# Tap weights from quarters of the TensorE array, kept in SBUF by ScalarE, with the products spread over the band

## The chip, the cores and the metric

One NeuronCore of a Trainium2 chip runs the whole kernel. The metric is the device time of one execution in microseconds. All data are float32.

## The reference, cut to what matters

Two layers work on an image batch x of 8 x 256 channels x 64 x 64. Each normalises x by groups (`_gn`) and adds its result to x. Layer 0 makes, for every pixel and every group of 8 channels, nine weights from a small network, and takes the weighted sum of the 3x3 neighbours of a value map x3. The change is in this layer:

```python
x1, x2, x3 = conv1x1(x, w1, b1), conv1x1(x, w2, b2), conv1x1(x, w3, b3)   # 32, 32, 256 channels
h = concat([x1, unfold3(reflect_pad(x2))])          # 32 + 9*32 maps
h = relu(bn2(conv1x1(relu(bn1(h)), cw1)))           # 32 maps
w = conv1x1(h, cw2, cb2).reshape(B, 32, 9, H, W)    # nine tap weights for each of 32 groups
x3u = unfold3(zero_pad(x3)).reshape(B, 32, 8, 9, H, W)
out = einsum('bgskhw,bgkhw->bgshw', x3u, w)         # 8 channels of a group share its weights
x = x + out
```

Layer 1 is a 7x7 local attention of four heads, plus a depthwise branch in which two depthwise 3x3 convolutions are weighted by a softmax over nine maps made from x (the matrix Wfc). It is left out here, since the change doesn't touch it.

## The kernel before

**Bands and steps.** An image is cut into 8 bands of 8 rows, so the batch has 64 bands. The main loop runs over g from -12 to 63. Pass g does layer 1 of band g, and, beside it, layer 0 of later bands: the maps of band g + 12 (`small_maps`, `value_maps`), the hidden maps of band g + 11 (`hidden_maps`), and the tap weights and products of band g + 10 (`tap_weights`). For g < -1 there is no layer 1 yet; the code calls these bands `alone`, and they are bands 0 to 8. The other 55 bands of tap weights are made beside layer 1, until g = 53. In the last ten passes layer 1 is alone.

**Order.** The whole order is written by hand (`manual_schedule`). A pass has 8 steps s, and a step has six places at which `advance()` runs what `after(n, f)` has deferred by n places; so a band has 48 places. Each engine executes its own queue in the order of issue. A pool tile with `bufs=n` is a ring: the next tile of that tag waits until the n-th before it has been read.

**Layer 0 in quarters.** For the tap weights a band of 8 rows is split into four quarters of 2 rows (SR = 2), and the 128 partitions are 4 quarters x 32 groups. h2 (the 32 hidden maps, `h2n`, two buffers, rows padded to HP = 66) therefore has 128 partitions x 132 elements. The weights matrix `c2` is block diagonal, four times the same 32x32 block, so that one 128x128 matmul per tap makes that tap's weights of all quarters:

```python
pw = ps.tile([P, n, SR * HP], F32, tag="gen", name=f"pw_{b}_{i}_{u}", bufs=4)
nc.tensor.matmul(pw[:, j], c2[:, first + j], h2n[i % 2]..., start=True, stop=True)
```

A matmul in float32 is two instructions, so a tap is two rows of the profile. Beside layer 1 the nine taps are made in five lots of 2, 2, 2, 2 and 1, at the end of steps 1 to 5 of the pass (`TAPS_AT`, `TG`). Each lot takes one of the four PSUM banks of tag `gen`, which it shares with most other results: pf (the Wfc maps, L886), ptp (transposed attention weights, L787), pq, pk, pv and p3. The score tiles sco (L750) and the tile small have banks of their own.

**Products.** One or two places after its lot, `product(j)` on VectorE (L483) adds the bias of tap k to its weight map in PSUM, and multiplies it, broadcast over the 8 channels of a group, with the shifted value map `x3q` in SBUF (128 x 1040). GpSimd then adds the product to `xg` (L491), which holds x. Products go through a ring of two tiles. After the ninth, VectorE takes statistics of xg, and it is written to DRAM as the input of layer 1.

**Other work on these engines.** VectorE also masks the scores (L764), makes the 8 other taps of each depthwise convolution (L843, L869, with their sums acc in PSUM), adds the attention results to xr (L818), and does the reciprocals of the softmax (L779, L907). GpSimd adds up the nine exponential maps (ex, L1106), and does the dynamic sum's other steps (L899, L902, L908, L912, L913). L912 and L913 read oc, the scaled depthwise result that ScalarE writes (L879), from a ring of two tiles. ScalarE makes all exponentials (L772, L891), empties most PSUM banks, and applies h2's Relu in `relu` (L441). DMAs beside layer 1 are issued by SP.

Of the kernel before, what the change touches and what calls it, by code (L numbers as in the profile page):

```python
# [10 lines left out]
F32 = mybir.dt.float32  # L11
BF16 = mybir.dt.bfloat16
AF = mybir.ActivationFunctionType
# [5 lines left out]
P = 128  # L19
C = 256  # L20
NCT = C // P
# [3 lines left out]
BAND = R * W  # L25
NB = H // R
# [4 lines left out]
REL = 32  # L31
KK = 9
# [3 lines left out]
SR = R // NQR  # L36
SHARE = C // REL
PIECE = SR * W
RUN = (SR - 1) * (W + 2) + W
TG = 2, 3  # L40
HP = W + 2
HR = R + 2

# [18 lines left out]
AHEAD = NB + 4  # L62
AHEAD0 = AHEAD + NB + 1
STEPS = NCT * NT // 2


TAPS_AT = (1, 2, 3, 4, 5), (0, 2, 4)
PRODUCTS_AT = ((1, 2),) * 5, ((7, 14, 10), (9, 17, 13), (12, 20, 16))


CB3, CBQ, CBK, CBP, CWP0, CWP1, CW1, CW2, CBV = 0, 1, 2, 3, 4, 5, 6, 15, 24
# [16 lines left out]
def conv_layers_kernel(ctx: ExitStack, tc: tile.TileContext, ins: dict, out: bass.AP):  # L88
    nc = tc.nc
    x_in = ins["x"]  # L90
    B = x_in.shape[0]

    const = ctx.enter_context(tc.tile_pool(name="const", bufs=1))
# [14 lines left out]
    def load(name, shape, src=None, now=True):  # L108
        t = const.tile(shape, F32, name=f"c_{name}")
        late.append(lambda: nc.scalar.dma_start(out=t, in_=ins[name] if src is None else src))  # L110
        if now:
            late.pop()()
        return t
# [8 lines left out]
    c1 = load("c1", [P, 3, REL])  # L122
    gq = load("gq", [P, P])
    gc = load("gc", [P, NCT, P])
    c2 = load("c2", [P, KK, P], now=False)
    wq = load("wq", [P, NCT, C], ins["wq"].rearrange("(t p) n -> p t n", p=P), now=False)
    wk = load("wk", [P, NCT, C], ins["wk"].rearrange("(t p) n -> p t n", p=P), now=False)
    wv = load("wv", [P, NCT, C], ins["wv"].rearrange("(t p) n -> p t n", p=P), now=False)
# [10 lines left out]
    x3n = [const.tile([P, R, HP], F32, name=f"x3n_{ct}") for ct in range(NCT)]  # L139

    h2n = [const.tile([P, SR, HP], F32, name=f"h2n_{i}") for i in range(2)]
    for t in probs + x3n + h2n:
        nc.gpsimd.memset(t, 0.0)

    def inverse_root(v):
# [45 lines left out]
    def layer1_loads():  # L191


        last = w1.tile([P, NCT, 1, C], F32, tag="oc", name="last")
        for f in late:
            f()
        nc.scalar.dma_start(out=last, in_=wfc_in[:, :, KK - 1 :])

        def first():
            nc.vector.tensor_scalar(wv, wv, rate1, None, ALU.mult)  # L200

        def difference(kt):
            nc.vector.tensor_sub(wfc[:, kt], wfc[:, kt], last[:, kt].to_broadcast([P, KK - 1, C]))

        return [first, lambda: difference(0), lambda: difference(1)]
# [205 lines left out]
    def hidden_maps(b, i, alone):  # L413

        im = images[b]
        hids = []
        h2 = h2n[i % 2][:, :, :W]

        def hidden(t):
            n = P if t == 0 else 96
            hid = w0.tile([P, R, W], F32, tag="hid", name=f"hid_{b}_{i}_{t}", bufs=2)
            nc.scalar.activation(
                hid[:n], im.x2[i][:n, t : t + R, :], AF.Relu, bias=bn1b[:n, t : t + 1], scale=bn1s[:n, t : t + 1]
            )
            hids.append(hid)

        def conv(home, first, last, start, stop):
            ph = home[:, 2 * P : 3 * P].rearrange("p (r c) -> p r c", r=SR)  # L430
            for t in range(first, last):
                n = P if t == 0 else 96
                for q in range(NQR):
                    nc.tensor.matmul(  # L434
                        ph[q * REL : (q + 1) * REL], c1[:n, t], hids[t][:n, q * SR : (q + 1) * SR],
                        start=(t == start), stop=(t == stop),
                    )
            return ph

        def relu(v):  # L440
            nc.scalar.activation(h2, v, AF.Relu, bias=bn2b, scale=bn2s)  # L441

        def one(home):
            ph = conv(home, 0, 2, 0, 1)
            after(1, lambda: hidden(2))
            after(2, lambda: nc.scalar.copy(h2, ph))

        def two(home):
            ph = conv(home, 2, 3, 2, 2)
            after(1, lambda: nc.vector.tensor_add(h2, ph, h2))  # L450
            after(3, lambda: relu(h2))

        hidden(0)
        after(3 if alone else 5, lambda: hidden(1))
        if alone:

            home = ps.tile([P, 4 * P], F32, tag="acc", name=f"ph_{b}_{i}")
            after(7, lambda: conv(home, 0, 2, 0, 2))
            after(8, lambda: hidden(2))
            after(12, lambda: after(4, lambda ph=conv(home, 2, 3, 0, 2): relu(ph)))  # L460
        return [two, one]

    def tap_weights(b, i, u, alone, at):


        im = images[b]
        first, n = TG[alone] * u, min(TG[alone], KK - TG[alone] * u)
        pw = ps.tile([P, n, SR * HP], F32, tag="gen", name=f"pw_{b}_{i}_{u}", bufs=4)
        for j in range(n):
            nc.tensor.matmul(  # L470
                pw[:, j], c2[:, first + j], h2n[i % 2].rearrange("p r c -> p (r c)"), start=True, stop=True
            )

        def product(j):
            k = first + j
            if alone and j == n - 1:
                prod = w1.tile([P, NCT, RP, W], F32, tag="yp", name=f"prod_{b}_{i}_{k}", bufs=3)
                prod = prod.rearrange("p t r c -> p (t r c)")[:, : SHARE * SR * HP]
                prod = prod.rearrange("p (s n) -> p s n", s=SHARE)
            else:  # L480
                prod = w0.tile([P, SHARE, SR * HP], F32, tag="prod", name=f"prod_{b}_{i}_{k}", bufs=2)
            at = k // 3 * HP + k % 3
            nc.vector.scalar_tensor_tensor(  # L483
                prod[:, :, :RUN], pw[:, j, :RUN].unsqueeze(1).to_broadcast([P, SHARE, RUN]),
                par[:, PCB2 + k : PCB2 + k + 1],
                im.x3q[i].rearrange("p s r c -> p s (r c)")[:, :, at : at + RUN], ALU.add, ALU.mult,
            )
            if alone and j == n - 1:
                after(9, lambda: gather(prod))
            else:  # L490
                nc.gpsimd.tensor_add(im.xg[i], im.xg[i], rows(prod))  # L491
            if k == KK - 2 + (not alone):
                if alone:
                    after(13, combine)
                after(14 if alone else 7, take)

        def rows(v):
            return v.rearrange("p s (r c) -> p s r c", c=HP)[..., :W]

        def gather(prod):  # L500
            if u == 0:
                im.part = score_tile(f"sum_{b}_{i}").rearrange("p t (s r c) -> p t s r c", r=SR, c=W)
            for t in range(2):
                nc.tensor.matmul(
                    im.part[:, t], ident, rows(prod)[:, t * SHARE // 2 : (t + 1) * SHARE // 2],
                    start=(u == 0), stop=(u == KK // n - 1),
                )

        def combine():
            x = im.xg[i].rearrange("p s r c -> p (s r c)")  # L510
            nc.vector.tensor_add(x, im.part.rearrange("p t s r c -> p (t s r c)"), x)

        def take():
            x = im.xg[i]
            if i == 0:
                im.st1 = stat.tile([P, 2 * NB, 6], F32, tag="st1", name=f"st1_{b}")
            for t in range(2):
                v = x[:, t * SHARE // 2 : (t + 1) * SHARE // 2].rearrange("p s r c -> p (s r c)")
                nc.vector.bn_stats(im.st1[:, 2 * i + t, :], v)
            im.x1[i] = dram.tile([C, BAND], F32, tag="x1", name=f"x1_{b}_{i}")  # L520
            if alone:
                after(9, lambda: keep(nc.scalar))
            else:
                keep(nc.sync)

        def keep(queue):
            for q in range(NQR):
                v = im.xg[i][q * REL : (q + 1) * REL].rearrange("p s r c -> p s (r c)")
                queue.dma_start(out=pieces(im.x1[i], q), in_=v)

        for j in range(n):
            after(at[j], lambda j=j: product(j))
# [133 lines left out]
    kept = {}  # L666
# [208 lines left out]

    def depthwise_end(b, i, ct, acc):

        oc = w1.tile([P, BAND], F32, tag="oc", name=f"oc_{b}_{i}_{ct}")
        nc.scalar.activation(oc, acc.rearrange("p r c -> p (r c)"), AF.Copy, scale=rate2)  # L879
        return oc  # L880

# [45 lines left out]
    def beside(g, s):  # L927
# [48 lines left out]
        alone = g < 0  # L976
# [8 lines left out]
        if 0 <= g + AHEAD - 1 < B * NB and s == (2 if alone else 1):  # L985
# [5 lines left out]
                    convs.extend(parts)  # L991

            end.append(hidden)
        if 0 <= g + AHEAD - 2 < B * NB and s in TAPS_AT[g < -1]:
            u = TAPS_AT[g < -1].index(s)
            end.append(
                lambda: tap_weights(*divmod(g + AHEAD - 2, NB), u, g < -1, PRODUCTS_AT[g < -1][u])
            )
        return head, mid, end

    def steer(g, s):
# [128 lines left out]
def _layout(inputs):  # L1130
# [29 lines left out]
    arr["par"] = par  # L1160

    c2 = a["a_cw2"].reshape(REL, KK, REL).transpose(2, 1, 0)
    arr["c2"] = np.zeros((P, KK, P), f)
    for q in range(NQR):
        arr["c2"][q * REL : (q + 1) * REL, :, q * REL : (q + 1) * REL] = c2

    chan = np.zeros((C, NCHAN), f)
    chan[:, CB3] = a["a_b3"]
# [43 lines left out]
```

## Time and profile before

| | |
|---|---|
| median of 3 runs | 3852.04 us (3850.59 to 3853.89) |
| profiled execution, its own time | 3854.63 us |
| its span in the profile | 3852.8 us |
| TensorE (PE) busy | 3756.3 us, 97% |
| VectorE (DVE) busy | 3434.4 us, 89% |
| GpSimd (POOL) busy | 3116.8 us, 81% |
| ScalarE (ACT) busy | 2809.2 us, 73% |
| mean granted TensorE clock | 0.994 |

Busy times are of one profiled execution. A group's row gives line, engine and operation, output and input by the program's names, shapes, the count, then busy time and mean nanoseconds of one, then the idle time of the engine in front of them with what ended most of it. In a timeline each row is a start, a length, the engine and the instructions that were merged into it. Bands are not marked in the profile: the steady part, with both layers at work, reaches from some 250 us to 3336 us.

### The profile page before, as it was taken

Reading aid. Unit: us, or ns where it says so; the run is one execution under the profiler, and the core shown is the slowest. Engines: PE = TensorE matmul, PEld = TensorE weight load, DVE = VectorE, ACT = ScalarE, POOL = GpSimd, SP = SyncE. Lnnn points to the kernel's source line nnn. Section 1 sums busy time; section 2 is a strip of 40 time slices with the busy share of each in tenths; the row PEclk is TensorE's granted clock in tenths of the full one; section 3 lists DMA queues with packets and bytes.
Section 4 is the critical chain, followed back from the end, with each engine's and each line's share of the span. In section 5 each row is a group of like instructions: output and inputs, shape, how many; then the busy total and the mean of one; then the engine's idle time right before and its main releaser. Section 6 shows DMA issues by size and latency. Waiting matters only on the chain.

```text
span 3852.8 us, 71646 instructions
## 1 busy us (share of the span) xinstructions
PE 3756.3 (97%) x24620; PEld 2109.9 (55%) x24620; DVE 3434.4 (89%) x7125; ACT 2809.2 (73%) x6770; POOL 3116.8 (81%) x2100
## 2 busy tenths in 40 slices
PE   6889999999999999999999999999999999999998
PEld 3445555555555555555555555555555555555554
DVE  6879999999999999899998999999999899978877
ACT  4457777777777777777777777777777777677776
POOL 4868888888897888888888888888888888855565
PEclk9999999999999999999999999999999999999999
DMA  8764544544444544544544544454544544232221
GB/s 247 210 177 128 142 118 129 151 126 118 133 135 131 145 123 115 148 135 127 136 116 142 142 125 120 126 149 125 136 115 117 138 119 114 74 97 78 79 67 37
DMA packets 438926, 490.14 MB, mean 127 GB/s; under 512 B 62016, under 2 KB 324256, under 8 KB 438304
## 3 DMA queue, kind: packets, MB, share of 16 engines
q1 hardware_dynamic: 421984, 469.79, 44.1%
q10 hardware_dynamic: 16576, 15.76, 1.3%
q8 instruction: 194, 3.18, 0.4%
q14 instruction: 172, 1.41, 0.1%
HBM read 343.76 MB, written 145.10 MB: 127 GB/s over the span
## 4 chain that ended last, share of the span: by engine, by line
PE 81%; POOL 10%; DVE 3%; DMA 2%; ACT 2%; issue 2%; SPq 1%; ACTq 0%; POOLq 0%; DVEq 0%
PE pf L886 39%; PE small L799 6%; PE ptp L787 6%; POOL xg L491 6%; PE pk L706 5%; PE pq L684 5%; PE sco L750 5%; PE p L375 5%; PE pv L601 5%; PE pw L470 2%; POOL ex L1106 2%; PE small L332 1%; DVE prod L483 1%; PE small L434 1%; DMA x<-x3n 1%
## 5 line engine op out<-in xcount | busy, mean ns | idle before, releaser
L886 PE MATMUL pf<-yp,c_wfc 128*128 128x512 f32 x4096 | 1916.8, 594 | 11.3 <-DVE prod L483 6.3
L491 POOL TENSOR_TENSOR xg<-xg,prod 128x1024 f32<-128x1024 f32 x549 | 1199.8, 2185 | 132.5 <-DVE prod L483 103.6
L886 PEld LDWEIGHTS pf<-yp,c_wfc 128*128 128x128 f32 x4096 | 739.6, 190 | 711.4 <-issue 654.7
L1106 POOL TENSOR_TENSOR ex<-ex,ex 128x1024 f32<-128x1024 f32 x384 | 908.8, 2367 | 68.5 <-ACT ex L891 65.0
L891 ACT ACTIVATE ex<-pf 128x512 f32<-128x512 f32 x1024 | 604.0, 590 | 347.9 <-PE pf L886 269.2
L843 DVE SCALAR_TENSOR_TENSOR acc<-yp,c_chan,acc 128x504 f32<-128x504 f32 (+3 forms) x1104 | 775.5, 702 | 63.2 <-ACT acc L834 42.8
L483 DVE SCALAR_TENSOR_TENSOR prod<-pw,c_par,x3q 128x1040 f32<-128x1040 f32 x576 | 732.7, 1294 | 107.9 <-PE pw L470 60.8
L869 DVE SCALAR_TENSOR_TENSOR acc<-hid,c_chan,acc 128x504 f32<-128x504 f32 (+3 forms) x1024 | 751.1, 733 | 18.1
L781 ACT ACTIVATE prob<-prob,tot 128x196 f32<-128x196 f32 x1024 | 412.9, 452 | 242.4 <-DVE tot L779 236.8
L772 ACT ACTIVATE prob<-prob,nmax 128x196 f32<-128x196 f32 x1024 | 458.2, 450 | 101.3 <-DVE nmax L764 101.2
L907 DVE RECIPROCAL rec<-tot 128x256 f32<-128x256 f32 x256 | 445.7, 1741 | 28.3 <-POOL tot L902 27.5
L789 ACT COPY pt<-ptp 112x512 f32<-112x512 f32 x511 | 295.9, 579 | 111.8 <-PE ptp L787 111.8
L764 DVE CUSTOM_DVE_ANT_0 prob<-sco,c_mask 128x196 f32<-128x196 f32 x1024 | 324.8, 355 | 31.0 <-PE sco L750 31.0
L787 PEld LDWEIGHTS ptp<-ident,prob 128*112 128x112 f32 x2044 | 227.3, 133 | 184.4 <-issue 132.7
L787 PE MATMUL ptp<-ident,prob 128*112 128x128 f32 x2044 | 319.5, 279 | 0.0
L908 POOL TENSOR_TENSOR tot<-tot,rec 128x256 f32<-128x256 f32 x254 | 185.8, 732 | 145.7 <-DVE rec L907 139.7
L799 PEld LDWEIGHTS small<-pt,vt 112*64 112x64 f32 x8144 | 258.6, 138 | 79.8 <-issue 60.5
L799 PE MATMUL small<-pt,vt 112*64 112x64 f32 x8144 | 294.2, 225 | 3.3 <-DMA vt<-vd 1.8
L601 PE MATMUL pv<-c_wv,yp 128*128 128x256 f32 x1056 | 253.5, 383 | 1.8 <-ACT yp L572 1.8
L902 POOL TENSOR_SCALAR tot<-tot 128x512 f32<-128x512 f32 x127 | 243.9, 1920 | 11.1
L470 PEld LDWEIGHTS pw<-h2n,c_c 128*128 128x128 f32 x1152 | 175.1, 191 | 139.9 <-issue 115.9
L375 PE MATMUL p<-xc,w3s 128*128 128x512 f32 x512 | 243.3, 598 | 0.0
(136 smaller groups left out, 4656.7 us busy)
## 6 DMA issues: line engine op xcount, KB each, us to landing
vt<-vd SPq DMA_DIRECT2D x512, 112.0 KB
x3q<-x SPq DMA_DIRECT2D x128, 264.0 KB
xc<-in_x SPq DMA_DIRECT2D x64, 512.0 KB
xg<-in_xg SPq DMA_DIRECT2D x64, 512.0 KB
yp<-x SPq DMA_DIRECT2D x128, 256.0 KB
xr<-x SPq DMA_DIRECT2D x64, 512.0 KB
out_x<-xr SPq DMA_DIRECT2D x64, 512.0 KB
xs<-in_x SPq DMA_DIRECT2D x57, 512.0 KB
```

Of the source, the lines that this page charges most:

```text
L483: nc.vector.scalar_tensor_tensor(prod[:, :, :RUN], pw[:, j, :RUN].unsqueeze(1).to_broadcast([P, SHARE, RUN]), par[:, PCB2 + k : PCB2 + k + 1],
L491: nc.gpsimd.tensor_add(im.xg[i], im.xg[i], rows(prod))
L601: nc.tensor.matmul(pv[:, g], yp[:, kt, r : r + 2].rearrange("p r c -> p (r c)"), wv[:, kt], start=(kt == 0), stop=(kt == NCT - 1),)
L772: nc.scalar.activation(prob[:, h, :NKEY], prob[:, h, :NKEY], AF.Exp, bias=nmax[:, h : h + 1], scale=-1.0, accum_out=tot[:, h : h + 1],)
L787: nc.tensor.transpose(ptp[:, h, ch], prob[:, h, ch * CHUNK : (ch + 1) * CHUNK], ident)
L799: nc.tensor.matmul(po[half[h], :, t * TQ : (t + 1) * TQ], im.vt[i + ch, m][:n, t, (2 * ct + h) * HD : (2 * ct + h + 1) * HD], pt[:n, h, ch ...
L843: nc.vector.scalar_tensor_tensor(o, yp[:, ct, ra + dr : rb + dr, ca + dc : cb + dc], chan[:, ct, CW1 + k : CW1 + k + 1], o, ALU.mult, ALU.add,
L869: nc.vector.scalar_tensor_tensor(o, hid[:, ra + dr : rb + dr, ca + dc : cb + dc], chan[:, ct, CW2 + k : CW2 + k + 1], o, ALU.mult, ALU.add,)
L886: nc.tensor.matmul(pf, wfc[:, kt, 2 * m + j, ct * P : (ct + 1) * P], images[b].yp[i][:, kt, PAD : PAD + R], start=(kt == 0), stop=(kt == N ...
L891: nc.scalar.activation(ex[:, j].rearrange("p (r c) -> p r c", r=R), pf, AF.Exp)
L907: nc.vector.reciprocal(rec, v)
L1106: after(4, lambda ex=ex, exb=exb: nc.gpsimd.tensor_add(ex, ex, exb))
```

## The change

The nine taps are made in two lots of 4 and 5 (`TAPS`), at the end of the last step of the pass before and of step 3 (`TAPS_AT`). Each matmul now uses a quarter of the array: 64 rows by 64 columns. A tap needs two of them, one for each half of its output partitions. Taps of a lot's first list use the upper 64 rows and write one PSUM bank, those of its second list use the lower 64 rows and write another, so that a tap needs both halves of h2 on the same 64 partitions. For that `relu` writes a second tile `h2s`, in which the halves of h2 are exchanged. `c2` shrinks to 64 columns.

Beside layer 1, ScalarE copies both banks of a lot to an SBUF tile `kept` (one buffer) one place later, and the products read their weights from there. They are spread over the band: 3, 8, 14 and 20 places after the first lot, 2, 5, 8, 11 and 14 after the second. For the 9 bands in front the products still read PSUM, at the places of before, and all their taps use the upper 64 rows.

The ring of tag `oc` goes from two tiles to one. In the diff, `...` marks what is left out.

```diff
-TG = 2, 3
+HALF = P // 2
...
-TAPS_AT = (1, 2, 3, 4, 5), (0, 2, 4)
-PRODUCTS_AT = ((1, 2),) * 5, ((7, 14, 10), (9, 17, 13), (12, 20, 16))
+TAPS = (((0, 1), (2, 3)), ((4, 5, 6), (7, 8))), tuple(((k, k + 1, k + 2), ()) for k in (0, 3, 6))
+TAPS_AT = (-1, 3), (0, 2, 4)
+PRODUCTS_AT = ((3, 8, 14, 20), (2, 5, 8, 11, 14)), ((7, 14, 10), (9, 17, 13), (12, 20, 16))
...
-    c2 = load("c2", [P, KK, P], now=False)
+    c2 = load("c2", [P, KK, HALF], now=False)
...
+    h2s = const.tile([P, SR, HP], F32, name="h2s")
-    for t in probs + x3n + h2n:
+    for t in probs + x3n + h2n + [h2s]:
         nc.gpsimd.memset(t, 0.0)
...
-        last = w1.tile([P, NCT, 1, C], F32, tag="oc", name="last")
+        last = w1.tile([P, NCT, 1, C], F32, tag="oc", name="last", bufs=1)
...
         def relu(v):
+            for a, z in ((0, HALF), (HALF, 0)):
+                o, z = slice(a, a + HALF), slice(z, z + HALF)
+                nc.scalar.activation(h2s[o, :, :W], v[z], AF.Relu, bias=bn2b[z], scale=bn2s[z])
             nc.scalar.activation(h2, v, AF.Relu, bias=bn2b, scale=bn2s)
...
-        first, n = TG[alone] * u, min(TG[alone], KK - TG[alone] * u)
-        pw = ps.tile([P, n, SR * HP], F32, tag="gen", name=f"pw_{b}_{i}_{u}", bufs=4)
-        for j in range(n):
-            nc.tensor.matmul(
-                pw[:, j], c2[:, first + j], h2n[i % 2].rearrange("p r c -> p (r c)"), start=True, stop=True
-            )
+        lots = TAPS[alone][u]
+        ks = [k for lot in lots for k in lot]
+        n = len(ks)
+        pws = [
+            ps.tile([P, len(lot), SR * HP], F32, tag="gen", name=f"pw_{b}_{i}_{u}_{r}", bufs=4)
+            for r, lot in enumerate(lots) if lot
+        ]
+        side = [slice(0, HALF), slice(HALF, P)]
+        for m in range(len(lots[0])):
+            for q in range(2):
+                for r, lot in enumerate(lots):
+                    if m < len(lot):
+                        h2 = (h2n[i % 2] if q == r else h2s)[side[r]].rearrange("p r c -> p (r c)")
+                        nc.tensor.matmul(pws[r][side[q], m], c2[side[r], lot[m]], h2, start=True, stop=True)
+        weights = [pw[:, m] for pw, lot in zip(pws, lots) for m in range(len(lot))]
+
+        def keep():
+            kept = w0.tile([P, KK - 4, SR * HP], F32, tag="pw", name=f"kept_{b}_{i}_{u}", bufs=1)
+            for pw, lot, at in zip(pws, lots, (0, len(lots[0]))):
+                nc.scalar.copy(kept[:, at : at + len(lot)], pw)
+            weights[:] = [kept[:, j] for j in range(n)]
+
+        if not alone:
+            after(1, keep)
...
             nc.vector.scalar_tensor_tensor(
-                prod[:, :, :RUN], pw[:, j, :RUN].unsqueeze(1).to_broadcast([P, SHARE, RUN]),
+                prod[:, :, :RUN], weights[j][:, :RUN].unsqueeze(1).to_broadcast([P, SHARE, RUN]),
                 par[:, PCB2 + k : PCB2 + k + 1],
                 im.x3q[i].rearrange("p s r c -> p s (r c)")[:, :, at : at + RUN], ALU.add, ALU.mult,
             )
...
-        oc = w1.tile([P, BAND], F32, tag="oc", name=f"oc_{b}_{i}_{ct}")
+        oc = w1.tile([P, BAND], F32, tag="oc", name=f"oc_{b}_{i}_{ct}", bufs=1)
...
-        if 0 <= g + AHEAD - 2 < B * NB and s in TAPS_AT[g < -1]:
-            u = TAPS_AT[g < -1].index(s)
-            end.append(
-                lambda: tap_weights(*divmod(g + AHEAD - 2, NB), u, g < -1, PRODUCTS_AT[g < -1][u])
-            )
+        for gt, st in ((g, s), (g + 1, s - STEPS)):
+            front = gt < -1
+            if 0 <= gt + AHEAD - 2 < B * NB and st in TAPS_AT[front]:
+                u = TAPS_AT[front].index(st)
+                end.append(
+                    lambda gt=gt, u=u, front=front: tap_weights(
+                        *divmod(gt + AHEAD - 2, NB), u, front, PRODUCTS_AT[front][u]
+                    )
+                )
```

More of the change, by code (lines that the diff above doesn't have):

```diff
@@ L466, in tap_weights @@
         im = images[b]
-        first, n = TG[alone] * u, min(TG[alone], KK - TG[alone] * u)
-        pw = ps.tile([P, n, SR * HP], F32, tag="gen", name=f"pw_{b}_{i}_{u}", bufs=4)
-        for j in range(n):
-            nc.tensor.matmul(
-                pw[:, j], c2[:, first + j], h2n[i % 2].rearrange("p r c -> p (r c)"), start=True, stop=True
-            )
+        lots = TAPS[alone][u]
[20 more added lines that the diff above has]
+            after(1, keep)
         def product(j):
-            k = first + j
+            k = ks[j]
             if alone and j == n - 1:
@@ L1162, in _layout @@
     c2 = a["a_cw2"].reshape(REL, KK, REL).transpose(2, 1, 0)
-    arr["c2"] = np.zeros((P, KK, P), f)
+    arr["c2"] = np.zeros((P, KK, HALF), f)
     for q in range(NQR):
-        arr["c2"][q * REL : (q + 1) * REL, :, q * REL : (q + 1) * REL] = c2
+        o = q * REL % HALF
+        arr["c2"][q * REL : (q + 1) * REL, :, o : o + REL] = c2
     chan = np.zeros((C, NCHAN), f)
```

## Prediction

> **What bounds the kernel now.** I read the page's busy line and chain first, to find the engine that sets the pace; then the windows of the steady part, for what the others have left.
>
> ```profile
> PE 3756.3 (97%) x24620; PEld 2109.9 (55%) x24620; DVE 3434.4 (89%) x7125; ACT 2809.2 (73%) x6770; POOL 3116.8 (81%) x2100
> PE 81%; POOL 10%; DVE 3%; DMA 2%; ACT 2%; issue 2%; SPq 1%; ACTq 0%; POOLq 0%; DVEq 0%
> PE pf L886 39%; PE small L799 6%; PE ptp L787 6%; POOL xg L491 6%; PE pk L706 5%; PE pq L684 5%; PE sco L750 5%; PE p L375 5%; PE pv L601 5%; PE pw L470 2%; POOL ex L1106 2%; PE small L332 1%; DVE prod L483 1%; PE small L434 1%; DMA x<-x3n 1%
> ```
>
> ```profile
> 1000.00:2000.00 1000.00, 994.98 (x6609) 563.01 (x6608) 921.46 (x1916) 757.33 (x1828) 855.78 (x575) 1.00 0.47 129
> 2000.00:3000.00 1000.00, 993.80 (x6682) 564.91 (x6681) 915.43 (x1910) 759.70 (x1838) 860.18 (x571) 1.00 0.48 131
> ```
>
> The windows' columns are busy time of PE, weight loads, DVE, ACT and POOL, then the granted clock. TensorE has 0.6% idle and is the bound. The tap weights (pw) are 2% of the chain. But DVE is at 92% and POOL at 86%. The group of the dynamic sum's first pass (L899 on POOL) starts first at 280.6 us, and the last pw matmul is at 3335.8, which is 53.3 bands later, so a band lasts **57.3 us**. Of that DVE has 4.7 us idle, POOL 8.1, ACT 13.8. The tail after 3336 us has no layer 0 work left. The change works on the 55 bands that are built beside layer 1; the 9 built in front keep products from PSUM.
>
> **What the Trainium skill says.** (1) "SBUF — State Buffer", section "Who interferes with whom": VectorE's second SBUF read goes through an interface that it shares with GpSimd. A VectorE instruction with two SBUF inputs and a GpSimd instruction that reads SBUF exclude each other for a whole instruction; one with at most one SBUF input does not contend. (2) "TensorEngine Tiling (Array Packing)", sections "Key Properties" and "Gotcha 1: PSUM Pressure": tiles run in parallel, different row tiles must write different PSUM banks, and a change of tiling mode drains the array.
>
> The trace agrees with (1). Nearly every long DVE row of this kernel has one operand in PSUM (pw, acc, sco, small, pk). The exception is L205, twice the same subtraction of 128x2048 from SBUF and SBUF. DVE first, then POOL:
>
> ```profile
> 55.60 4.20 DVE L205 TENSOR_TENSOR c_wfc<-c_wfc,last 128x2048 f32<-128x2048 f32 x1
> 71.55 2.28 DVE L205 TENSOR_TENSOR c_wfc<-c_wfc,last 128x2048 f32<-128x2048 f32 x1
> ```
>
> ```profile
> 50.97 6.68 POOL L491 TENSOR_TENSOR xg<-xg,prod 128x1024 f32<-128x1024 f32 x3
> 68.66 2.17 POOL L491 TENSOR_TENSOR xg<-xg,prod 128x1024 f32<-128x1024 f32 x1
> 75.19 11.23 POOL L491 TENSOR_TENSOR xg<-xg,prod 128x1024 f32<-128x1024 f32 x5 [4.36 <-DVE prod L483]
> ```
>
> The second runs 71.55 to 73.83, with POOL idle from 70.83 to 75.19: 2.28 us. The first starts while POOL is in the third of three additions, which ends at 57.65. It takes 4.20 us: 55.60 plus a wait to 57.52, plus 2.28. So it stood still until POOL was done. That is one case of DVE held by POOL; POOL held by DVE is not in the trace, only in the page of the skill.
>
> The trace agrees with (2) too. These are TensorE's rows of pw beside the scores, which use 64x64 quarters with two row and two column halves:
>
> ```profile
> 2000.24 0.61 PE L470 MATMUL pw<-h2n,c_c 128*128 128x132 f32 x4
> 2000.79 0.92 PE L750 MATMUL sco<-kb,qb 64*64 64x196 f32 x16
> 2001.64 1.15 PE L799 MATMUL small<-pt,vt 112*64 112x64 f32 x32
> ...
> 2008.94 0.61 PE L470 MATMUL pw<-h2n,c_c 128*128 128x132 f32 x4
> 2009.39 1.88 PE L886 MATMUL pf<-yp,c_wfc 128*128 128x512 f32 x4
> ```
>
> From start to next start, 4 full-array pw instructions take 0.45 us before a pf and 0.55 before the scores, so a switch costs 0.1. The 16 score instructions take 0.85 us.
>
> **The change, part by part, for one band.**
>
> *TensorE.* Removed: 18 instructions of 128x132, in lots of 4, 4, 4, 4, 2: 18/4 x 0.45 = 2.03 us. Added: 36 quarter instructions, in lots of 16 and 20. Scaled from the scores by columns, 0.85 x 132/196 = 0.57 us for 16, 0.72 for 20: 1.29 us. Both lots now stand right ahead of a score stage, in its mode, so the count of switches is the same. Gain 0.74 us a band, x 55 = **41 us**. If the price is per instruction and not per column (0.85/16 = 53 ns), 36 take 1.91 and the gain is 0.12 a band, 7 us. If it falls with the columns without the scores' overhead, 1.0 us a band, 55 us. TensorE's gain counts only while it stays the bound.
>
> *ScalarE.* Added: two 64-row Relu copies into h2s (the nearest row, L441 of 128x128, takes 482 ns each) and four copies PSUM to SBUF. The 128x256 row of L608 has 359 ns and its 128x512 row 569, so 0.82 ns a column: three of 264 columns at 366 and one of 396 at 474. Sum 0.96 + 1.57 = 2.5 us a band, 43.5 to 46.0 of 57.3. It lies in ACT's idle time. Queued behind a kept copy are the next pt and the exponentials. The kept tile has one buffer: the second copy needs the fourth product of the first lot to be done, some 5 of the band's 48 places earlier. The oc tile falls to one buffer too: its ACT write must follow POOL's L913. In the trace of before POOL's end comes 1.15 to 4.5 us ahead of that write (600 to 1200 us), so it costs nothing now, but any delay of POOL beyond that stops ACT, and with it the exponentials that free pf's banks.
>
> *DVE and POOL.* The count of products (9 of 128x1040, 1.21 us from start to start) and of POOL additions is unchanged, and SP's transfers keep their order; the first product comes 10 places earlier in the band, and in the trace x3q made a product wait 0.7 us in all, so I cost that at nothing; the halved load of c2 and one more clearing of a tile lie at the start, under other loads. What is new is that **both tensor inputs of a product, kept and x3q, lie in SBUF**. By the rule above it then takes turns with POOL, whose long rows all read SBUF:
>
> ```profile
> L491 POOL TENSOR_TENSOR xg<-xg,prod 128x1024 f32<-128x1024 f32 x549 | 1199.8, 2185 | 132.5 <-DVE prod L483 103.6
> L1106 POOL TENSOR_TENSOR ex<-ex,ex 128x1024 f32<-128x1024 f32 x384 | 908.8, 2367 | 68.5 <-ACT ex L891 65.0
> L483 DVE SCALAR_TENSOR_TENSOR prod<-pw,c_par,x3q 128x1040 f32<-128x1040 f32 x576 | 732.7, 1294 | 107.9 <-PE pw L470 60.8
> ```
>
> Two stretches of 600 us of the timelines hold 192 products: at 93% of their starts POOL was inside an instruction, with 0.84 us of it left on average over all. So DVE gets 9 x 0.84 = 7.6 us a band of standing. POOL gets up to 9 x 1.21 = 10.9. Against the idle time: DVE 7.6 - 4.7 = +2.9 us if it uses up every gap; the shared interface 49.2 + 10.9 = 60.1, +2.8. Neither can use every gap, since each still waits for the other's results (POOL's idle time in front of L908, 139.7 us in all, ends on DVE's reciprocal). I let DVE keep half of its idle time: 7.6 - 2.35 = **+5.2 us a band**, x 55 = 289 us. Low end: half of the waits escape (the products are spread): 3.8 us fits in the idle time, and some +0.7 a band is left, +40 us. High end: nothing is absorbed and oc's buffer stalls ACT: +8 a band, +440 us. Who is behind the standing product: the masking of the scores (L764), the taps of acc and the additions of xr, and so the exponentials, ptp and the scores' banks: DVE's delay reaches TensorE.
>
> Sum: TensorE's 41 us vanish under the new bound; the profiled execution was 3854.6 us (span 3852.8), the median 3852.0. 3852 + 289 = **4141**, stated as 4140.
>
> **Rivals.**
> (a) *TensorE's gain is the result.* If two SBUF streams of this form do not exclude POOL, or products fall into POOL's gaps, DVE and POOL stay under 57 us and the end follows TensorE: 3852 - 41 = 3811 us. For it: TensorE is at 99.4%, DVE and POOL are not. Against: L205, and POOL free at only 7% of product starts. It decides if a product costs DVE under about 0.5 us of standing. 0.14.
> (b) *No exclusion, but the single buffers of oc and kept hold ACT.* Two waits a band of 1 us beyond the slack of 1.15 us give +110, less 41: 3920. Against: POOL ends early enough now. 0.06.
> (c) *The quarters do not overlap.* 36 x 110 ns (pitch of 132 columns) = 3.96 us, +1.9 a band, 3958 us without exclusion. The scores' 53 ns against 196 columns speak against it. Under 0.01, counted with (b).
> (d) *It evens out*: the waits just eat the gain, 3852. 0.02.
>
> **How the numbers follow.** Exclusion as bound 0.78, giving 3890 to 4300; slower in all with (b) 0.84, faster 0.14, same 0.02, where the bound of 0.2% is what a measurement of this kernel can tell from no change. The range is that of the likeliest case, whose ends also take in (b); (a) and a rest above 4300 stay outside.
>
> **What would show it.** Right: the products' mean in the DVE groups rises from 1294 ns to some 2100, with a wide spread between min and max; the POOL additions grow too; TensorE's busy share falls to some 90% with idle time in front of sco and pf; a band of 62 us to 3600 us and unchanged bands after; oc's ACT write waits on POOL. pw should take about 1.3 us a band. Wrong: products that keep 1.29 us while POOL works, or TensorE still at 99%.

## Result and the profile after

The changed kernel takes **4183.23 us** (4179.77 to 4193.3, 4 runs) against 3851.7 us before: ratio **1.0863**, 95% interval 1.0844 to 1.0881. The profiled execution has a span of 4184.6 us, 331.8 more than before.

The page of the changed kernel, busy line and chain:

```profile
PE 3829.2 (92%) x25772; PEld 2060.3 (49%) x25772; DVE 3723.9 (89%) x7125; ACT 2921.5 (70%) x7118; POOL 3320.2 (79%) x2101
DVE 36%; PE 24%; POOL 15%; ACT 14%; issue 7%; DMA 4%; SPq 1%; ACTq 0%; POOLq 0%; DVEq 0%
DVE prod L506 13%; PE pf L909 12%; POOL xg L514 7%; DVE acc L892 7%; DVE rec L930 4%; DVE acc L866 4%; POOL ex L1133 3%; POOL tot L922 3%; PE small L822 2%; DVE prob L787 2%; ACT x L349 2%; PE sco L773 2%; POOL tot L925 2%; ACT prob L804 2%; DMA yp<-x 2%
```

Its windows of the steady part, columns as before:

```profile
1000.00:2000.00 1000.00, 920.12 (x6298) 496.71 (x6297) 911.83 (x1746) 719.39 (x1763) 828.48 (x521) 0.97 0.44 120
2000.00:3000.00 1000.00, 918.81 (x6251) 494.85 (x6251) 911.60 (x1729) 712.03 (x1746) 831.93 (x517) 0.97 0.44 119
```

TensorE fell from 99.4% to 92%, and the chain moved: products (L506) are now its first line. No engine is full. The granted clock is 0.97 in these windows, against 1.00 before, and a pf row took 612 ns on average instead of 594; how much that adds to the time was not tested. From the first dynamic sum of band 0 (279.8 us) to that of band 53 (3658.6) a band lasts **63.75 us**. Counted the same way in the kernel before (280.6 to 3333.4) it lasted 57.60. The difference of 6.15 us over 53 bands is 326 of the 332 us. The groups of the changed kernel:

```profile
L514 POOL TENSOR_TENSOR xg<-xg,prod 128x1024 f32<-128x1024 f32 x549 | 1212.5, 2209 | 470.9 <-DVE prod L506 439.5
L506 DVE SCALAR_TENSOR_TENSOR prod<-kept,c_par,x3q 128x1040 f32<-128x1040 f32 x495 | 947.5, 1914 | 101.4 <-POOL xg L514 67.1
L925 POOL TENSOR_SCALAR tot<-tot 128x512 f32<-128x512 f32 x127 | 319.7, 2518 | 11.1
L922 POOL TENSOR_TENSOR tot<-ex 128x512 f32<-128x512 f32 x127 | 212.8, 1676 | 10.0
```

The last two, steps of the dynamic sum, in the kernel before:

```profile
L902 POOL TENSOR_SCALAR tot<-tot 128x512 f32<-128x512 f32 x127 | 243.9, 1920 | 11.1
L899 POOL TENSOR_TENSOR tot<-ex 128x512 f32<-128x512 f32 x127 | 161.7, 1273 | 9.9
```

The products of the front, in the groups with shapes kept apart:

```profile
L506 DVE SCALAR_TENSOR_TENSOR prod<-pw,c_par,x3q 128x1040 f32<-128x1040 f32 x81 | 100.9, 1291 | 19.0 <-DMA x3q<-x 7.3 <-PE pw L485 5.1 <-POOL xg L514 4.7
```

The 495 products from SBUF have a mean of 1914 ns; the 81 of the front, still from PSUM, 1291. L925 grew from 1920 to 2518 ns and L922 from 1273 to 1676 with the same work. The additions of xg, at 2185 ns before, grew only to 2209. The timeline shows both sides holding each other, DVE first:

```profile
1999.74 2.82 DVE L506 SCALAR_TENSOR_TENSOR prod<-kept,c_par,x3q 128x1040 f32<-128x1040 f32 x1
...
2003.30 1.50 DVE L506 SCALAR_TENSOR_TENSOR prod<-kept,c_par,x3q 128x1040 f32<-128x1040 f32 x1
...
2008.88 3.31 DVE L506 SCALAR_TENSOR_TENSOR prod<-kept,c_par,x3q 128x1040 f32<-128x1040 f32 x1 [1.07 <-POOL xg L514]
```

```profile
1999.10 2.37 POOL L1133 TENSOR_TENSOR ex<-ex,ex 128x1024 f32<-128x1024 f32 x1
2001.54 2.15 POOL L922 TENSOR_TENSOR tot<-ex 128x512 f32<-128x512 f32 x1
2003.78 2.79 POOL L925 TENSOR_SCALAR tot<-tot 128x512 f32<-128x512 f32 x1
2006.65 4.45 POOL L514 TENSOR_TENSOR xg<-xg,prod 128x1024 f32<-128x1024 f32 x2
```

The first product starts 1.73 us before L1133 ends (2001.47) and takes 2.82 = 1.29 + 1.73 - 0.20. L922 starts while that product runs, 1.02 us before its end, and takes 2.15 instead of 1.27, 0.88 more. L925 starts 1.02 us before the second product's end and takes 0.87 more. The third product's row starts 0.04 us ahead of the second of the two additions, and it stands for 2.0 us; which of two that begin so close together goes first can't be told from their starts. In the other cases here whichever starts second stands until 0.14 to 0.2 us before the other ends. L925 is an exception on one side. It is held by a product, but holds a product only at its own beginning:

```profile
1264.05 1.92 POOL L925 TENSOR_SCALAR tot<-tot 128x512 f32<-128x512 f32 x1
```

```profile
1265.12 1.30 DVE L506 SCALAR_TENSOR_TENSOR prod<-kept,c_par,x3q 128x1040 f32<-128x1040 f32 x1
```

This product starts 1.07 us after L925, which has 0.85 us left, and does not stand at all. In the traces of all runs with products from SBUF, 82 products start inside this instruction. The seven that start in its first 0.4 us stand until 0.41 us after its start; the other 75 take at most 1.304 us.

What the delay does further is in the waits of the changed kernel (total, times, longest):

```profile
ACT prob L804 <- DVE tot L802: 500.1, 306, 3.8
ACT prob L795 <- DVE nmax L787: 358.0, 148, 5.6
DVE prod L506 <- ACT kept L491: 34.4, 43, 1.4
```

In the kernel before:

```profile
ACT prob L781 <- DVE tot L779: 236.8, 202, 2.6
ACT prob L772 <- DVE nmax L764: 101.2, 111, 4.8
```

ScalarE waits for maxima and reciprocals that stand behind products in VectorE's queue. There is no wait of oc's ACT write on POOL.

### The profile page after: what moved, and what is told of

The parts are those of the page before. It is cut to its first block, busy times and chain, and to the rows that moved or that the text cites. A ratio compares the mean times of both kernels' runs of the same rounds, so it can differ in the third digit from the quotient of the medians.

```text
span 4184.6 us, 74172 instructions
## 1 busy us (share of the span) xinstructions
PE 3829.2 (92%) x25772; PEld 2060.3 (49%) x25772; DVE 3723.9 (89%) x7125; ACT 2921.5 (70%) x7118; POOL 3320.2 (79%) x2101
## 4 chain that ended last, share of the span: by engine, by line
DVE 36%; PE 24%; POOL 15%; ACT 14%; issue 7%; DMA 4%; SPq 1%; ACTq 0%; POOLq 0%; DVEq 0%
DVE prod L506 13%; PE pf L909 12%; POOL xg L514 7%; DVE acc L892 7%; DVE rec L930 4%; DVE acc L866 4%; POOL ex L1133 3%; POOL tot L922 3%; PE small L822 2%; DVE prob L787 2%; ACT x L349 2%; PE sco L773 2%; POOL tot L925 2%; ACT prob L804 2%; DMA yp<-x 2%
## 5 line engine op out<-in xcount | busy, mean ns | idle before, releaser
L909 PE MATMUL pf<-yp,c_wfc 128*128 128x512 f32 x4096 | 1976.0, 612 | 103.8 <-ACT ex L914 103.8
L514 POOL TENSOR_TENSOR xg<-xg,prod 128x1024 f32<-128x1024 f32 x549 | 1212.5, 2209 | 470.9 <-DVE prod L506 439.5
L909 PEld LDWEIGHTS pf<-yp,c_wfc 128*128 128x128 f32 x4096 | 758.4, 194 | 865.8 <-issue 653.7
L506 DVE SCALAR_TENSOR_TENSOR prod<-kept,c_par,x3q 128x1040 f32<-128x1040 f32 x495 | 947.5, 1914 | 101.4 <-POOL xg L514 67.1
L1133 POOL TENSOR_TENSOR ex<-ex,ex 128x1024 f32<-128x1024 f32 x384 | 907.4, 2363 | 68.4 <-ACT ex L914 64.6
L925 POOL TENSOR_SCALAR tot<-tot 128x512 f32<-128x512 f32 x127 | 319.7, 2518 | 11.1
L931 POOL TENSOR_TENSOR tot<-tot,rec 128x256 f32<-128x256 f32 x254 | 199.8, 787 | 151.7 <-DVE rec L930 145.6
L707 PE MATMUL pq<-yp,c_wq 128*128 128x512 f32 x512 | 242.0, 595 | 13.4 <-ACT ex L914 9.4
```

The source lines that it names most:

```text
L506: nc.vector.scalar_tensor_tensor(prod[:, :, :RUN], weights[j][:, :RUN].unsqueeze(1).to_broadcast([P, SHARE, RUN]), par[:, PCB2 + k : PCB2 ...
L909: nc.tensor.matmul(pf, wfc[:, kt, 2 * m + j, ct * P : (ct + 1) * P], images[b].yp[i][:, kt, PAD : PAD + R], start=(kt == 0), stop=(kt == N ...
L1133: after(4, lambda ex=ex, exb=exb: nc.gpsimd.tensor_add(ex, ex, exb))
```

## Experiments

Ratios are to the kernel before on the same chip. Theory A: products with two SBUF inputs and GpSimd exclude each other, and that is the loss. Its rivals: ScalarE's copies and the single buffers; the quarters; and, once e2 had come back, theory B, the products' places in VectorE's queue.

### e1: the quarters alone

```diff
-TAPS = (((0, 1), (2, 3)), ((4, 5, 6), (7, 8))), ...
-TAPS_AT = (-1, 3), (0, 2, 4)
+TAPS = (((0,), (1,)), ((2,), (3,)), ((4,), (5,)), ((6,), (7,)), ((8,), ())), ...
+TAPS_AT = (1, 2, 3, 4, 5), (0, 2, 4)
-PRODUCTS_AT = ((3, 8, 14, 20), (2, 5, 8, 11, 14)), ...
+PRODUCTS_AT = ((1, 2),) * 5, ...
-        if not alone:
-            after(1, keep)
-... tag="oc" ..., bufs=1)      (twice)
+... tag="oc" ...)
```

> The quarters alone: five lots of 2, 2, 2, 2, 1 taps at the places of before, each tap pair on the upper and lower 64 rows with two PSUM banks, h2s written, products read PSUM, no kept copies, oc ring of two. Theory (a product with two SBUF inputs takes turns with GpSimd, and that is the whole loss): nothing contends, TensorE stays the bound and its gain comes out: 3795 to 3835 us, products at 1.29 us, pw at 1.3 to 1.5 us a band. Rival 1 (quarters do not overlap, or their mode switches and second bank cost TensorE): 3870 us or more. Rival 2 (h2s and more PSUM banks per lot hold other engines): 3850 to 3900 us with waits on the gen banks.

Measured: 3857.22 us, ratio 1.0008 (0.9998 to 1.0018). Neither the gain nor a loss. From start to next start between 600 and 1800 us, pw fell from 2.37 to 1.83 us a band, but pf rose from 27.66 to 28.22. TensorE's timeline of e1 shows why:

```profile
2002.07 1.88 PE L906 MATMUL pf<-yp,c_wfc 128*128 128x512 f32 x4
2003.88 0.32 PE L485 MATMUL pw<-h2n,c_c 64*64 64x132 f32 x1
...
2004.26 1.98 PE L906 MATMUL pf<-yp,c_wfc 128*128 128x512 f32 x4
```

Four pf instructions ahead of quarters take 1.81 us from start to start, against 1.72 between full-array work, and the lot 0.38: together 0.02 more than before's 1.72 + 0.45. A lot between pf and pf pays two switches of mode, into quarters and back, for its saving. The quarters in these lots don't explain the loss.

### e2, e3, e4: copies, then SBUF products, in the kernel before

```diff
-PRODUCTS_AT = ((1, 2),) * 5, ...
+PRODUCTS_AT = ((2, 3),) * 5, ...
+        weights = [pw[:, j] for j in range(n)]
+        def keep():
+            kept = w0.tile([P, 2, SR * HP], F32, tag="pw", ..., bufs=2)
+            nc.scalar.copy(kept[:, :n], pw)
+            weights[:] = [kept[:, j] for j in range(n)]     # e3 and e4; in e2: pass
+        if not alone:                                       # e4: and u in (1, 3)
+            after(1, keep)
...
-... tag="oc" ...)      (twice, in all three)
+... tag="oc" ..., bufs=1)
```

> Before plus ScalarE's copies of every pw bank to SBUF beside layer 1 (five a band), but the products still read PSUM, 2 and 3 places after the lot; oc ring of one. Theory: the copies and the single oc buffer are covered by ScalarE's idle time: 3840 to 3875 us. Rival (ScalarE's added work and the single buffers make the loss): 3950 us or more.

> The same kernel as e2 with one difference: the nine products of a band beside layer 1 read the copy in SBUF. Full-array tap weights, products in pairs. Theory: the whole loss comes back without quarters or spreading: 4080 to 4280 us, mean product 1.8 to 2.2 us. Rival (loss from quarters, spreading or buffers): as e2, within 1%.

> As e3, but only the four products of the second and fourth lot of a band read the SBUF copy; the other five read PSUM and have no copy. Theory: the loss grows with the count of such products, a little less than 4/9 of e3's if idle time of VectorE takes some first: 3890 to 4020 us. Rival (a threshold: VectorE's 4.7 us of idle time a band cover four waits of some 0.6 us): 3840 to 3880 us.

Measured: e2 4130.36 us, ratio 1.0715 (1.0699 to 1.0731); e3 4557.34, 1.1829 (1.1809 to 1.1849); e4 4334.93, 1.1246 (1.1229 to 1.1263). All three are above what theory A expected. In e2 the products keep 1298 ns (median), so 275 us are lost with no exclusion at all; theory A alone was not enough, and the move by one place, made to give the copy time, became a suspect (e6). Between e2 and e3 only the source differs, and that alone is 427 us. In e4 four of nine products read SBUF; it lies 205 us above e2, with three copies a band fewer.

### e5: the places alone

The kernel before, with the changed kernel's product places:

```diff
-TG = 2, 3
+LOTS = ((0,), (1,), (2,), (3,), (4, 5), (6, 7), (8,)), ...
-TAPS_AT = (1, 2, 3, 4, 5), (0, 2, 4)
-PRODUCTS_AT = ((1, 2),) * 5, ...
+TAPS_AT = (-1, 0, 1, 2, 3, 4, 5), (0, 2, 4)
+PRODUCTS_AT = ((3,), (2,), (2,), (2,), (2, 5), (2, 5), (2,)), ...
```

(with the changed kernel's loop that lets a lot stand in the pass before)

> Before with the changed kernel's product places: full-array tap weights in seven lots of 1, 1, 1, 1, 2, 2, 1, no copies, products read PSUM. VectorE's and GpSimd's queues are then those of the changed kernel (8 of 576 products stand one place off). Theory A (exclusion by the SBUF source is the loss): 3840 to 3900 us. Theory B (the order of the products on VectorE is a large part of the loss, as e2 made possible: there products stand ahead of the softmax reciprocals): 4000 us or more.

Measured: 3886.66 us, ratio 1.0078 (1.0061 to 1.0095). Its product group:

```profile
L483 DVE SCALAR_TENSOR_TENSOR prod<-pw,c_par,x3q 128x1040 f32<-128x1040 f32 x576 | 742.3, 1295 | 101.8 <-POOL xg L491 77.4 <-PE pw L470 11.1 <-POOL x L357 6.8
```

The places cost 30 us, not 330. With the queues of VectorE and GpSimd as in the changed kernel, a PSUM source gives 1295 ns where an SBUF source gives 1914.

### e6: one place later

```diff
-PRODUCTS_AT = ((1, 2),) * 5, ...
+PRODUCTS_AT = ((2, 3),) * 5, ...
```

> Before with one number changed: the products stand 2 and 3 places after their lot and not 1 and 2, so that the second of a lot is ahead of the reciprocal of the attention sums (L779). No copies, oc ring of two. If e2's 275 us come from the order: 4050 us or more, with ScalarE's prob waiting long for DVE's tot. If they come from the copies, which tie each product to ScalarE's queue: 3850 to 3900 us.

Measured: 4058.21 us, ratio 1.0528 (1.0502 to 1.0554). The first of the two waits above, 236.8 us in the kernel before, is in e6:

```profile
ACT prob L781 <- DVE tot L779: 704.9, 302, 6.0
```

So most of e2's loss was the place: a product ahead of the small reciprocal holds the softmax. e2 to e4 share that place, so only their differences count. e2 adds 72 us to e6 for the copies and oc's ring.

### e7: GpSimd without the additions

```diff
-            else:
+            elif alone:
                 nc.gpsimd.tensor_add(im.xg[i], im.xg[i], rows(prod))
```

> The changed kernel without GpSimd's additions of the products to xg beside layer 1 (the result lacks those terms); all products are still made from SBUF at the same places. GpSimd is then in an instruction for about half of the time. Theory A: products wait half as often, 0.3 us on average, which fits into VectorE's idle time: 3810 to 3900 us, mean product 1.5 to 1.65 us. Theory B (order of VectorE's queue): the order is kept, so 4100 us or more.

The kernel leaves nine additions a band out, so its result lacks these terms. Measured: 3999.84 us, ratio 1.0372 (1.0357 to 1.0388): some 185 us come back, but both theories missed. The products of e7:

```profile
L506 DVE SCALAR_TENSOR_TENSOR prod<-kept,c_par,x3q 128x1040 f32<-128x1040 f32 x495 | 901.8, 1822 | 50.8 <-ACT kept L491 48.7 <-POOL xg L514 2.1
```

1822 ns is hardly less than 1914. Of 150 products between 1000 and 2000 us, 54 found GpSimd idle and took 1.30 us, and so did 17 that began inside L925. But 48 met an addition of ex (L1133), where the changed kernel has 17 of 141, and stood for 1.38 us on average. GpSimd's new idle time was not where the products stood. Theory A's mechanism holds row by row; its assumption that waits follow the busy share does not.

### e8: the changed kernel at the old places

```diff
-PRODUCTS_AT = ((3, 8, 14, 20), (2, 5, 8, 11, 14)), ...
+PRODUCTS_AT = ((13, 14, 19, 20), (1, 2, 7, 8, 13)), ...
```

> The changed kernel with its products back at the places of before (in pairs); quarters, copies and SBUF source stay. Theory A: the exclusion stays, and pairs meet GpSimd's addition of the first product: 4150 to 4350 us. Theory B (the new places are the loss): 3850 to 3950 us.

Measured: 4354.77 us, ratio 1.1295 (1.1278 to 1.1312), mean product 2180 ns. With SBUF weights spreading helps, by some 170 us: in pairs the second product meets the addition of the first. Between 1000 and 2000 us, 48 of e8's 135 products began inside an addition of xg (L514) or less than 0.1 us ahead of it, where the changed kernel has 22 of 141.

### e9, e10: one difference at the new places

Both are e5 with the `keep` of e2 and e3 (seven copies a band, none read in e9, all read in e10) and an oc ring of one.

```diff
 e9:   nc.scalar.copy(kept[:, :n], pw); pass
 e10:  nc.scalar.copy(kept[:, :n], pw); weights[:] = [kept[:, j] for j in range(n)]
```

> e5 (the changed kernel's product places, full-array tap weights, products from PSUM) plus ScalarE's copies of each pw bank to SBUF beside layer 1 and an oc ring of one; the products still read PSUM. Theory A (exclusion): the copies cost what e2 cost over e6 at most, 72 us: 3880 to 3970 us. Rival (copies and single buffers are the larger part of what the changed kernel loses beyond e5's 30 us): 4050 us or more.

> As e9 with one difference: the products beside layer 1 read the copy in SBUF. Theory A: the loss of the changed kernel is back, 4120 to 4280 us, mean product 1.8 to 2.1 us, and its difference to e9 is 200 us or more. Rival: within 60 us of e9.

Measured: e9 4001.56 us, ratio 1.0383 (1.0367 to 1.0399); e10 4296.93, 1.115 (1.1135 to 1.1165). First e9's row, then e10's:

```profile
L493 DVE SCALAR_TENSOR_TENSOR prod<-pw,c_par,x3q 128x1040 f32<-128x1040 f32 x576 | 743.3, 1297 | 314.3 <-ACT kept L478 213.8 <-POOL xg L501 67.4 <-PE pw L470 14.2
```

```profile
L493 DVE SCALAR_TENSOR_TENSOR prod<-kept,c_par,x3q 128x1040 f32<-128x1040 f32 x495 | 954.9, 1929 | 295.8 <-ACT kept L478 228.3 <-POOL xg L501 67.0
```

**The source alone is 295 us**, with all that follows from it; the granted clock, too, is 0.981 in e10 and 0.992 in e9. The rest of e9, 115 us over e5, goes with VectorE's wait for ScalarE's copy one place earlier, 213.8 us in e9 (its products read PSUM, yet the trace has them released by the copy). That this wait makes the 115 us is argued, not shown. In the changed kernel, with four copies a band and, but for one product, two or more places between copy and product, that wait is 34.4 us.

### e11, e12: quarters where they pay

e1 with lots only ahead of score stages, products from PSUM:

```diff
 e11:
+TAPS = (((0, 1), (2,)), ((3, 4), (5,)), ((6, 7), (8,))), ...
+TAPS_AT = (1, 3, 5), ...
+PRODUCTS_AT = ((1, 2, 5),) * 3, ...
 e12:
+TAPS = (((0,), (1,)), ((2,), (3,)), ((4, 5), (6,)), ((7,), (8,))), ...
+TAPS_AT = (-1, 1, 3, 5), ...
+PRODUCTS_AT = ((1, 2), (1, 2), (1, 2, 5), (1, 2)), ...
```

> e1 (quarters, PSUM products, no copies) with three lots of three taps at the end of steps 1, 3 and 5, each just ahead of a score stage that uses quarters too, and products 1, 2 and 5 places later. If e1's gain was eaten by mode switches around lots that stand between full-array work (pf took 0.36 us a band more there), three lots without such a place gain 0.8 to 1.1 us a band on TensorE: 3795 to 3840 us. If the products' order or the banks held longer cost as much as in e5: 3850 to 3900 us.

> e1 with four lots of 2, 2, 3, 2 taps, each just ahead of a score stage (end of the last step of the pass before, and of steps 1, 3 and 5), products from PSUM 1 and 2 places later, as before, and one 5 places later. TensorE's pw falls by 0.9 to 1.1 us a band and the switches around lots in full-array work are gone. If only one product stands where e11's three did, most of that gain comes out: 3810 to 3845 us. If pairs of products at a step's start are themselves the cost once there are fewer steps to hold them: 3850 to 3890 us.

Measured: e11 3878.98 us, ratio 1.0066 (1.0054 to 1.0079); e12 **3819.39 us, ratio 0.9906** (0.9889 to 0.9924), 0.9% faster than the kernel before. pw is 1.21 us a band in e11 and 1.24 in e12, against 2.37 before. In e11 TensorE is at 98%: its gain went into waits. e12's chain and a window:

```profile
PE 85%; DVE 5%; ACT 4%; POOL 2%; DMA 2%; issue 1%; SPq 1%; ACTq 0%; POOLq 0%; DVEq 0%
```

```profile
1000.00:2000.00 1000.00, 993.75 (x7093) 549.67 (x7091) 934.47 (x1954) 787.60 (x1892) 872.66 (x583) 1.00 0.48 132
```

TensorE is back at 99.4% and sets the time. 35 us come out with these four lots; the prediction worked out 41 for the two of the changed kernel.

## Why the prediction was right, point by point

- **The direction and its cause** hold. 4183 stands against 4140. The exclusion, read from the two L205 rows and "SBUF — State Buffer", "Who interferes with whom", is in the trace row by row, now in both directions, and e9 against e10 puts 295 us on it at the new places. In the changed kernel itself it can't be separated so cleanly: 30 us belong to the places (e5), and the copies' share was not measured apart. In two points the page and the prediction's rendering of it need a limit. L925 holds a product for 0.41 us and not for the whole instruction; there the measurement decides. And the page exempts an instruction with at most one SBUF input only outside VectorE's two-port modes, a condition that the prediction left out; here the products from PSUM kept 1.29 to 1.30 us beside a busy GpSimd.
- **The wait of one product** was put too high: 0.84 us, measured 1914 - 1290 = 0.62, or 5.6 us a band instead of 7.6. The average came from before's places, where most products met a busy GpSimd. By the recorded starts it was 86% of them, with 0.78 us left on average; if a GpSimd instruction that begins less than 0.1 us later counts as met too, it was 97%, with 0.99 us. At the new places 38 of 141 products (1000 to 2000 us) found it idle. At the old places e8 has 2180 - 1290 = 0.89 us.
- **Half of VectorE's idle time was to absorb it**; none did. Idle was 4.7 us a band and is now 5.6 (63.75 x 0.088). Its gaps are ends of other waits, not a reserve. This error and the one above nearly cancel: +5.2 us a band predicted, +6.15 measured. That the total came so close was luck in part.
- **The band of 57.3 us** was read with 53.3 bands to the last pw matmul; 53.0 pass, so it was 57.6. This shifts the sum by less than 1%.
- **GpSimd** was held for less than the 10.9 us that I gave as a limit: its busy time rose by 203 us, 3.7 a band. The sign that its additions of products grow hardly came (2185 to 2209 ns); L925, L922 and L936, the last step of the dynamic sum, took 162 of the 203 us.
- **The places were not priced.** I checked only x3q's arrival. They cost 30 us here, but e6 shows that one place can cost 200. It is the term that the sum lacked.
- **ScalarE's copies were put at nothing.** VectorE waits 34.4 us for them in the changed kernel, so the term was small there. With seven copies, six of them one place ahead of a product, the same wait is 213.8 us (e9), and that kernel stands at 4002 us, above the 3920 of rival (b).
- **oc's single buffer** was to make ScalarE wait for GpSimd. It did not.
- **TensorE's price** of the two lots, 1.29 us a band, was measured at 1.33 (600 to 1800 us, start to next start); what they replace, put at 2.03, takes 2.37 in the kernel before, switches to the scores' mode included. The gain was hidden, as forecast; that quarters can bring such a gain is shown by e12's 35 us. But e1 shows that it hangs on where the lots stand; the switches of "TensorEngine Tiling (Array Packing)", "Key Properties", cost 0.09 to 0.1 us each.

## What to carry to other kernels

Before moving an operand from PSUM to SBUF, look at the VectorE instruction that reads it: if its other tensor input is in SBUF and GpSimd works beside it, expect the two engines to stand for each other, as they did here. What such waits cost depends on what GpSimd is doing at those places (in e7 it did less, and the mean product fell only from 1914 to 1822 ns), so read the neighbours in the timeline and not the busy share. Put array quarters next to work that uses the same quarters, and before you move a long instruction in a full queue, see which small one will then stand behind it.

## What was not expected of the hardware

The exclusion is exact enough to calculate with. In the six traces with products from SBUF (the changed kernel, e3, e4, e7, e8 and e10) 1632 of these products begin with more than 0.2 us of a GpSimd instruction left. Of them 1489 take 1.29 us plus what is left of it minus 0.17 to 0.21 us. The others have a pattern too: 76 begin inside L925; 30 begin inside a clearing of x3q, which reads no tensor, and 12 of these take 1.30 us, while 18 stand for what comes right behind it; and 37 products of e8 stand through the next GpSimd instruction as well. GpSimd's held instructions grow by what is left of the product minus 0.11 to 0.15 us in most cases. L925 is held like the others, to 0.14 us before the product's end, but lets a product pass from 0.41 us after its own start, though it lasts 1.92; why, no run shows. And alone, a product from SBUF and SBUF takes hardly longer than one from PSUM: 1.30 us with GpSimd idle, 1.29 from PSUM.
